# Layer 3 of a four-layer kernel: the shared expert and the second pair's projections written ahead of the expert blocks, and the sum of the state spaces kept in place

## The chip, the cores and the metric

The kernel runs on one core of a Trainium2 chip. The metric is device time in microseconds; the kernel before takes 1370.8 us, the median of three runs that reached from 1363.27 to 1372.84. "PE" is the matrix engine, "DVE" the vector engine, "ACT" the scalar engine, "POOL" the engine that also issues the indirect transfers, "SP" the queue that issues the plain ones. A matmul writes into PSUM banks[...].

## The reference, cut to what matters

Four layers follow one another on 2048 tokens of width 128. Each takes `xn = layernorm(x)`, computes a sequence mixer `s` and a gate `g` from it, and sets `x = x + s * g`. Only layer 3 is touched:

```
xn = _layernorm(x)
# mixer: two Mamba2 halves, forward on xn[:64], backward on xn[64:], 2 heads of 64, state 128
h  = rmsnorm(xn) * norm_w
zxbcdt = u @ in_w.T                      # u: one half of h
xBC = silu(conv4(xBC) + conv_b);  dt = softplus(dt + dt_bias)
scan: state = exp(dt*A)*state + (dt*x) B^T ;  y = state C
y = rmsnorm((y + D*x) * silu(z)) * gnorm_w ;  out_half = y @ outp_w.T
s = xn + concat(out_f, out_b) @ op_w.T + op_b
# gate: 16 experts of width 64, the best 2 of each token, and one shared expert of width 128
moe    = sum over the 2 best: w_k * (silu(xn @ gate_k) * (xn @ up_k)) @ down_k
shared = (silu(xn @ sh_gate.T) * (xn @ sh_up.T)) @ sh_down.T
x = x + s * silu(moe + shared)
```

The sum in `s` starts from `xn` itself, since the mixer has a residual: `s = xn + op_b + forward half + backward half`.

## The kernel before, in words

**Tiling.** Tokens lie in 16 tiles of 128 rows (`NT = 16`), four tiles to a group (`G = 4`, `NG = 4` groups), eight tiles to each of the two sequences. `x`, `xn` and `xT` (the transpose of `xn`, features on partitions) live through the whole kernel.

**Preparation (L1650 to L1685).** For each group the layer norm is written into `xn` (L1657), SP copies the group to DRAM as `xs` (`keep_rows`, L1219), ACT scales it into `xw` (L1665), POOL copies half of it (L1666), PE transposes `xn` into `xT` and `xw` into `X`, one array for each direction, shifted for the convolution. `plg` holds the router's logits and the step sizes.

**Routing (L1686 to L1693).** `top2` picks two experts of each token. `Dispatch` (L1086) turns that into blocks of 128 rows with one expert each, 47 blocks. It is a long chain of small DVE operations that ends in a large one-hot table `dhh` (L1162 on DVE, then a product on POOL, L1163), eight one-hot tables `dla` on DVE (L1170, in two buffers, borrowed from the state space's `uda`), and 32 matmuls into one bank, `pinv` (L1172, recorded as L287). From `pinv` come the row lists `dto` and `dfrom`.

**Sums.** `s` is a tile of its own in pool `a3`. POOL writes `s = xn + op_b` into it for each group (L1697). Each state-space unit later adds its output with `gated` (L1700).

**State space.** A pair is one group of tiles in both directions: `pairs[0]` to `pairs[3]`. For each pair, `stacked` computes the input projections: 24 matmuls into `px` (six banks) and 4 into `pz`, each bank followed by a SiLU on ACT into `uxs` or `usz` (L462, L472). `unit` computes the rest for one direction: `uda` -> `pd` -> exp `uE` (L545 to L548), `pe` (L557), transposes `pt`, `uxdt`, `uxst`, `pcb`, `ucb`, the product `uE` (L581), the states `pst` (L601), `py`, `pi`, `uy`, `pss`, a root (L300), `pyo`, and `gated`. `together` advances several of these generators in turn. With `busy=True` (the first three pairs) the elementwise products go to DVE, in the last pair to POOL. `uxs` has four buffers, so two pairs' projections can exist at a time.

**Blocks (L1721 to L1756).** Twelve groups of up to four blocks. For each block POOL issues an indirect gather `xb <- xs` (L1188), SP fetches the expert's weights `tw` (L1194); PE transposes (`pxb`), multiplies (`pgb`), ACT and DVE make the gated product, PE transposes (`phb`) and multiplies (`pob`), and POOL issues an indirect scatter `ys <- yb` (L1198). `xb` has two buffers of four blocks.

**Shared expert (L1757 to L1771).** For each group two matmuls of 512 columns (`pgt`, `put`), a SiLU on ACT (L1766), a product on DVE (L1767, `hT`), four matmuls into `psh`, and a copy into `acc`, which by turns goes to ACT (L282) or DVE (L284).

**End (L1774 to L1779).** For each group, `fetch` reads the two rows of each token back from `ys` (`yt`, after all scatters), adds them into `acc` on DVE (L398), then SiLU (L1776), `acc * s` (L1777), `x + acc` (L1778), and the store (L1779).

**What sets the order.** A scheduler lays out each engine's queue when the program is built: what is written earlier goes first among what it holds to be ready, and each engine then runs its queue strictly in that order, whatever is ready on the chip. PSUM banks come from two pools of four, and banks of one pool are handed out as they come free: `sa3` serves `px`, `pz`, `pc` and the units; `sf3` serves `pinv`, the blocks and the shared expert. So both streams advance side by side.

Of the kernel before, what the change touches and what calls it, by code (L numbers as in the profile page):

```python
# [10 lines left out]
F32 = mybir.dt.float32  # L11
F32R = mybir.dt.float32r
I32 = mybir.dt.int32
AF = mybir.ActivationFunctionType
# [5 lines left out]
P = 128  # L20
NB, SEQ = 2, 1024
T = NB * SEQ
NT = T // P
TPB = SEQ // P
G = 4
NG = NT // G
# [616 lines left out]
def together(*parts):  # L643

    live = list(parts)
    while live:
        live = [p for p in live if next(p, p) is not p]


def grp(a, g):  # L650
    return a[:, g * G : (g + 1) * G, :]
# [971 lines left out]
def layer3(K, x, xn, xT, w, inp, out):  # L1623
    nc, tc, c = K.nc, K.tc, K.c
    four = [P, G, P]
    with ExitStack() as es:
        pa = es.enter_context(tc.tile_pool(name="a3", bufs=1))
        pf = es.enter_context(tc.tile_pool(name="f3", bufs=1))
        sa = es.enter_context(tc.tile_pool(name="sa3", bufs=4, space=PSUM))
        sf = es.enter_context(tc.tile_pool(name="sf3", bufs=4, space=PSUM))  # L1630
# [61 lines left out]
            d = Dispatch(K, pf, pr, sf, h1, h2, 16, P, inp["lists"], ((pa, "uxs", 4, 1536), (pa, "uda", 2)))  # L1692
            w12 = K.pair_softmax(pf, m1, m2)  # L1693
        pe = es.enter_context(tc.tile_pool(name="e3", bufs=1))
        s0 = pa.tile([P, NT, P], F32, name="s")
        for g in range(NG):
            nc.gpsimd.tensor_add(grp(s0, g), grp(xn, g), w["opb"].unsqueeze(1).to_broadcast(four))  # L1697

# [12 lines left out]
        space = StateSpace(K, pa, sa, parts)  # L1711
        pairs = [[(m, b, n) for m in parts] for b in range(NB) for n in range(TPB // G)]
        together(space.stacked(pairs[0]))
        space.steps(pdt)
        together(*(space.unit(*u, busy=True) for u in pairs[0]), space.stacked(pairs[1]))
        loaded = {}

        def load_rows(n0):
# [5 lines left out]
        for n0 in range(0, d.n, 4):  # L1724
# [16 lines left out]
            sg = pf.tile([P, 4, 64], F32, name="sgb", bufs=2)[:, :m, :]  # L1741
# [8 lines left out]
            po = sf.tile(four, F32, name="pob", tag="ps")[:, :m, :]  # L1750
# [3 lines left out]
            K.copy(yb, po)  # L1754
            for r, n in enumerate(part):
                d.store(yb[:, r, :], n)  # L1756
        acc = pe.tile([P, NT, P], F32, name="acc")  # L1757
        for g in range(NG):
            rhs = xT[:, g * 512 : (g + 1) * 512]
            pgt = sf.tile([P, 512], F32, name="pgt", tag="ps")  # L1760
            put = sf.tile([P, 512], F32, name="put", tag="ps")
            K.mm(pgt, w["sg"], rhs)
            K.mm(put, w["su"], rhs)
            sg = pf.tile([P, 512], F32, name="sg", bufs=2)
            hT = pf.tile([P, 512], F32, name="hT", bufs=2)
            nc.scalar.activation(sg, pgt, AF.Silu)  # L1766
            nc.vector.tensor_mul(hT, sg, put)  # L1767
            po = sf.tile(four, F32, name="psh", tag="ps")
            for j in range(G):
                K.mm(po[:, j, :], hT[:, j * P : (j + 1) * P], w["sd"])  # L1770
            K.copy(grp(acc, g), po)  # L1771
        for n, p in enumerate(pairs[1:]):
            together(*(space.unit(*u, busy=n < 2) for u in p), *(space.stacked(q) for q in pairs[n + 2 : n + 3]))
        for g in range(NG):  # L1774
# [7 lines left out]
def build(tc, io, packs):  # L1782
    nc = tc.nc
    with ExitStack() as ctx:
        pool = ctx.enter_context(tc.tile_pool(name="const", bufs=1))
        x = pool.tile([P, NT, P], F32, name="x")
        src = io["x"].rearrange("b (t p) d -> p (b t) d", p=P)
        for g in range(NG):
            nc.sync.dma_start(grp(x, g), src[:, g * G : (g + 1) * G, :])
        xn = pool.tile([P, NT, P], F32, name="xn")  # L1790
        xT = pool.tile([P, T], F32, name="xT")

        def load(into, n, by=nc.scalar):
            t = into.tile([P, packs[n].n], F32, name="w_" + n)
            by.dma_start(t, io[n])
            return View(t, packs[n])

        K = Kern(tc, load(pool, "c"))
        dram = ctx.enter_context(tc.tile_pool(name="lists", bufs=1, space=DRAM))
        lists = {n: dram.tile([rows, P], F32, name=n) for n, rows in (("xs", T), ("ys", 2 * T))}  # L1800
        views = {}
        with tc.tile_pool(name="const0", bufs=1) as pool0:
            w0 = load(pool0, "l0")
            e0 = load(pool0, "e0")
            layer0(K, x, xn, xT, w0, e0)
        later = ctx.enter_context(tc.tile_pool(name="const3", bufs=1))
        views["l3"] = load(later, "l3")
        pair = lists["xs"], lists["ys"]
        with tc.tile_pool(name="const2", bufs=1) as pool0:
            views.update((n, load(pool0, n)) for n in ("l1", "l2"))  # L1810
            layer1(K, x, xn, xT, views["l1"], {"rows": io["rows1"], "lists": pair, **{n: io[n] for n in ("sw1", "sw3", "sw2")}})
            layer2(K, x, xn, xT, views["l2"], {"rows": io["rows2"], "lists": pair})
        layer3(K, x, xn, xT, views["l3"], {"load": lambda pool: load(pool, "x3", nc.sync), "rows": io["rows3"], "lists": pair}, io["out"].rearrange("b (t p) d -> p (b t) d", p=P))
# [17 lines left out]
```

## Time and profile before

| what | value |
|---|---|
| median of 3 runs | 1370.8 us (1363.27 to 1372.84) |
| the profiled execution | 1371.2 us, its span 1369.3 us |
| mean granted clock of PE | 0.887 |
| busy in the span: PE, DVE, ACT, POOL | 1134.2, 885.1, 634.7, 425.2 us |
| matmuls, first `px` of layer 3 | starts at 1148.0 us |
| PE between `pz` and the first `pinv` | idle for 10.05 us, from 1161.5 to 1171.5 us |
| first and last scatter or gather of layer 3 on POOL | 1181.7 and 1322.9 us |
| shared expert on PE | 1319.3 to 1342.5 us |
| last addition of a unit's output | 1363.8 us |

The span runs from the first to the last instruction, and the time is taken around it: it is 1.9 us longer in the profiled execution. Each engine's busy time is that of its own instructions; matmuls overlap, so a busy PE may still have room. A table of stretches gives for each engine the busy time within a stretch and the number of instructions, and the clock that PE was granted. In a list in order of time, a bracket says how long the engine had been idle before the line, and what released it.

### The profile page before, as it was taken

The page shows a single profiled execution, that of the slowest core. Times are in us where ns is not written, and L with a number is a line of the kernel's source. Part 1 is how long each engine was busy: PE and PEld are TensorE (multiplying, and loading weights), DVE is VectorE, ACT ScalarE, POOL GpSimd, SP SyncE. Part 2 cuts the span into 40 slices and gives each one's busy share as a digit, 9 for nine tenths or more (in the row PEclk, how much of TensorE's full clock was granted, in tenths as well). Part 3 has the DMA queues.
Part 4 walks back from the last instruction along what each step waited for, and adds up shares of the span by engine and source line. Part 5 has one row for each costly group of instructions (what it writes and reads, how often), then busy time and mean ns, then how long its engine had stood idle before and what let it go on. Part 6 is the DMA issues. An engine that isn't in the chain of part 4 may idle for free. (4 is left out here: it accounts for less than half of the span.)

```text
span 1369.3 us, 19321 instructions
## 1 busy us (share of the span) xinstructions
PE 1134.2 (83%) x6861; PEld 793.5 (58%) x6861; DVE 885.1 (65%) x2216; ACT 634.7 (46%) x1072; POOL 425.2 (31%) x420
## 2 busy tenths in 40 slices
PE   5599866888898748999999998679989918799985
PEld 2277455787798425544444433458778815577664
DVE  6536445875665686577787753988657469566456
ACT  7665926215413232344455576233452316355761
POOL 0352160027455150000000000034766521467743
PEclk9899885899999757699999998769999967799997
DMA  2000003014344200000000000024344530233411
GB/s 89 0 1 1 0 15 122 1 59 157 105 136 134 62 0 1 1 1 1 1 1 1 1 1 24 8 89 117 111 131 126 155 104 24 70 85 96 78 54 47
DMA packets 49040, 75.72 MB, mean 55 GB/s; under 512 B 7335, under 2 KB 36402, under 8 KB 48688
## 3 DMA queue, kind: packets, MB, share of 16 engines
q1 hardware_dynamic: 39632, 54.30, 12.7%
q0 software_dynamic: 8448, 14.98, 5.0%
q10 hardware_dynamic: 864, 5.21, 1.1%
q8 instruction: 54, 0.88, 0.3%
q14 instruction: 42, 0.34, 0.1%
HBM read 63.95 MB, written 12.85 MB: 56 GB/s over the span
## 5 line engine op out<-in xcount | busy, mean ns | idle before, releaser
L1424 DVE TENSOR_REDUCE mx<-pm 128x1 f32<-128x512 f32 (+3 forms) x304 | 182.1, 656 | 65.6 <-PE pm L287 62.6
L1468 ACT ACTIVATE pr<-psc 128x1024 f32<-128x1024 f32 x144 | 139.6, 1021 | 103.9 <-PE psc L287 68.2
L1188 POOL DMA_INDIRECT xb<-xs,dfrom x132 | 131.7, 998 | 123.2 <-PE pxb L797 31.5
L1198 POOL DMA_INDIRECT ys<-yb,dto x132 | 137.0, 1038 | 95.3 <-DVE yb L1076 44.4
L1163 POOL TENSOR_TENSOR dhh<-dhh,w_c 128x1280 fp32r<-128x1280 f32 (+2 forms) x3 | 8.8, 2927 | 480.3 <-issue 385.6
L287 PE MATMUL pm<-kT,qT 32*128 32x128 f32 (+3 forms) x576 | 119.3, 364 | 15.5 <-DVE mx L1424 11.4
L287 PEld LDWEIGHTS pm<-kT,qT 32*128 32x128 f32 x576 | 68.8, 203 | 68.3 <-DVE mx L1424 48.2
L287 PE MATMUL p<-xbT,tw 128*128 128x256 f32 x368 | 100.6, 391 | 1.7 <-ACT sg L1069 1.4
L1069 ACT ACTIVATE sg<-p,tw 128x256 f32<-128x256 f32 x92 | 40.8, 472 | 94.9 <-PE p L287 87.2
L287 PE MATMUL pat<-pr,va 128*32 128x512 f32 x576 | 81.0, 630 | 0.2 <-ACT pr L1468 0.2
L293 PE MATMUL tp<-w_c,xn 128*128 128x128 f32 x64 | 19.5, 412 | 67.7 <-DVE xn L325 40.3
L287 PEld LDWEIGHTS p<-xbT,tw 128*128 128x128 f32 x368 | 63.4, 194 | 12.3 <-ACT sg L1069 3.5
L287 PE MATMUL psc<-qT,kT 32*128 32x512 f32 x288 | 64.8, 487 | 3.0 <-ACT pr L1468 3.0
L1070 DVE SCALAR_TENSOR_TENSOR hh<-p,tw,sg 128x256 f32<-128x256 f32 x92 | 42.6, 479 | 35.6 <-ACT sg L1069 24.0
L287 PEld LDWEIGHTS po<-tw,hh 128*128 128x128 f32 x368 | 54.6, 193 | 5.8 <-DVE hh L1070 1.1
L287 PE MATMUL po<-tw,hh 128*128 128x128 f32 x368 | 56.7, 277 | 0.4 <-DVE hh L1070 0.4
L293 PEld LDWEIGHTS tp<-w_c,xn 128*128 128x128 f32 x64 | 11.5, 187 | 75.8 <-issue 38.7
L287 PE MATMUL psc<-mT,onesR 32*128 32x512 f32 x288 | 54.5, 410 | 0.0
L282 ACT COPY xbT<-pxb 128x256 f32<-128x256 f32 (+3 forms) x38 | 15.2, 401 | 61.0 <-PE pxb L797 44.9
L287 PEld LDWEIGHTS psc<-qT,kT 32*128 32x128 f32 x288 | 31.4, 188 | 15.9 <-ACT pr L1468 13.6
L287 PE MATMUL pcum<-kv,w_c 128*128 128x512 f32 x64 | 35.3, 652 | 2.1 <-DVE prod L1286 1.6
L287 PE MATMUL pd<-uda,w_c 128*128 128x512 f32 x64 | 34.9, 647 | 0.9 <-ACT usz L517 0.9
(531 smaller groups left out, 2840.6 us busy)
## 6 DMA issues: line engine op xcount, KB each, us to landing
tw<-in_rows SPq DMA_DIRECT2D x23, 836.0 KB, 4.8
tw<-in_rows SPq DMA_DIRECT2D x39, 384.0 KB, 3.2
yt<-ys SPq DMA_DIRECT2D x24, 256.0 KB, 3.0
tw<-in_rows SPq DMA_DIRECT2D x47, 128.0 KB, 2.2
xb<-xs,dfrom POOLq DMA_INDIRECT x132, 3.3
ys<-yb,dto POOLq DMA_INDIRECT x132, 2.3
xs<-xn SPq DMA_DIRECT2D x8, 256.0 KB, 2.3
w_l<-in_l ACTq DMA_DIRECT2D x1, 1890.0 KB, 11.1
```

What stands on the lines that cost most here:

```text
L282: self.nc.scalar.copy(out, in_)
L287: self.nc.tensor.matmul(out, lhsT=lhsT, rhs=rhs, start=start, stop=stop)
L293: self.nc.tensor.transpose(pt[:, j, :], src(g * G + j), self.c["ident"])
L1069: nc.scalar.activation(sg, p1[:, k - k0, :], AF.Silu, bias=t[:, 1536 + k : 1537 + k])
L1070: nc.vector.scalar_tensor_tensor(hh[:, k, :], p2[:, k - k0, :], t[:, 1540 + k : 1541 + k], sg, ALU.add, ALU.mult)
L1163: nc.gpsimd.tensor_mul(h, h.bitcast(F32), c["slot"][:, at].unsqueeze(2).to_broadcast(shape))
L1188: self.K.nc.gpsimd.indirect_dma_start(dst, None, self.xs, bass.IndirectOffsetOnAxis(self.of_token[:, n : n + 1], 0))
L1198: d = self.K.nc.gpsimd.indirect_dma_start(self.ys, bass.IndirectOffsetOnAxis(self.to[:, n : n + 1], 0), src, None, bounds_check=2 * T - 1, ...
L1424: nc.vector.tensor_reduce(mx[:, starts.index(a), g, j : j + k], tile[0][:, : k * m].rearrange("p (j m) -> p j m", m=m), AX.X, ALU.max)
L1468: K.nc.scalar.activation(pr, ps, AF.Exp, scale=scale)
```

## The change

Four things are changed in `layer3`, and nothing elsewhere.

1. `s0` is now `xn` itself: POOL adds `op_b` to `xn` in place, and the units add their outputs into `xn`. The tile `s` is gone.
2. `stacked(pairs[1])` was advanced together with the two units of `pairs[0]`; it is now written ahead of them, alone, right after `space.steps`.
3. The shared expert's loop is written after that, ahead of the units of `pairs[0]` and of all blocks; before, it came after the last block. Its operations are the same, in the same pool of PSUM banks.
4. `acc` comes from pool `a3` instead of `e3`, and the copy of `psh` is always ACT's.

```
-        s0 = pa.tile([P, NT, P], F32, name="s")
+        s0 = xn
         for g in range(NG):
             nc.gpsimd.tensor_add(grp(s0, g), grp(xn, g), w["opb"].unsqueeze(1).to_broadcast(four))
...
         together(space.stacked(pairs[0]))
         space.steps(pdt)
-        together(*(space.unit(*u, busy=True) for u in pairs[0]), space.stacked(pairs[1]))
+        together(space.stacked(pairs[1]))
+
+        acc = pa.tile([P, NT, P], F32, name="acc")
+        for g in range(NG):
+            rhs = xT[:, g * 512 : (g + 1) * 512]
+            pgt = sf.tile([P, 512], F32, name="pgt", tag="ps")
+            put = sf.tile([P, 512], F32, name="put", tag="ps")
+            K.mm(pgt, w["sg"], rhs)
+            K.mm(put, w["su"], rhs)
+            sg = pf.tile([P, 512], F32, name="sg", bufs=2)
+            hT = pf.tile([P, 512], F32, name="hT", bufs=2)
+            nc.scalar.activation(sg, pgt, AF.Silu)
+            nc.vector.tensor_mul(hT, sg, put)
+            po = sf.tile(four, F32, name="psh", tag="ps")
+            for j in range(G):
+                K.mm(po[:, j, :], hT[:, j * P : (j + 1) * P], w["sd"])
+            nc.scalar.copy(grp(acc, g), po)
+        together(*(space.unit(*u, busy=True) for u in pairs[0]))
         loaded = {}
...
             for r, n in enumerate(part):
                 d.store(yb[:, r, :], n)
-        acc = pe.tile([P, NT, P], F32, name="acc")
-        for g in range(NG):
-            rhs = xT[:, g * 512 : (g + 1) * 512]
...
-            K.copy(grp(acc, g), po)
         for n, p in enumerate(pairs[1:]):
```

More of the change, by code (lines that the diff above doesn't have):

```diff
@@ L1756, in layer3 @@
                 d.store(yb[:, r, :], n)
-        acc = pe.tile([P, NT, P], F32, name="acc")
-        for g in range(NG):
-            rhs = xT[:, g * 512 : (g + 1) * 512]
[L1760 to L1770, printed above, removed]
-            K.copy(grp(acc, g), po)
         for n, p in enumerate(pairs[1:]):
```

## The prediction, made before the result was known

> **What bounds the kernel now.** I first read the row of slices for PE and its clock, then a table of stretches of layer 3, then PE's, POOL's, ACT's and DVE's lists in order of time where PE was idle. The slices say that PE is the fullest engine, with dips at the layers' starts and ends; the change lies in the last six or seven slices.
>
> ```profile
> PE   5599866888898748999999998679989918799985
> PEclk9899885899999757699999998769999967799997
> ```
>
> The stretches cut layer 3 at its own events (columns: stretch; length; busy time and number for PE, weight load, DVE, ACT, POOL; PE's clock; DMA).
>
> ```profile
> 1161.50:1171.50 10.00, 0.00 (x0) 0.00 (x0) 9.83 (x23) 2.36 (x3) 3.14 (x1) 0.67 0.25 75
> 1171.50:1180.50 9.00, 8.98 (x40) 8.78 (x41) 5.35 (x8) 0.28 (x1) 0.00 (x0) 0.50 0.33 92
> 1180.50:1227.80 47.30, 45.77 (x268) 31.97 (x268) 24.59 (x59) 26.92 (x38) 31.08 (x32) 0.95 0.28 74
> 1227.80:1272.90 45.10, 42.88 (x273) 31.05 (x273) 25.81 (x59) 27.99 (x41) 32.78 (x33) 1.00 0.33 92
> 1272.90:1318.50 45.60, 42.69 (x269) 30.69 (x269) 24.89 (x62) 28.00 (x41) 32.86 (x33) 1.00 0.34 49
> 1318.50:1343.50 25.00, 21.65 (x134) 15.81 (x134) 16.52 (x40) 14.85 (x20) 11.30 (x10) 1.00 0.36 102
> 1343.50:1369.30 25.80, 11.31 (x66) 10.36 (x64) 13.49 (x39) 4.21 (x7) 5.80 (x5) 0.68 0.08 25
> ```
>
> Three things are to be seen. PE does nothing for 10 us while DVE routes. In the next 9 us it is called busy, but at half clock. From 1180.5 to 1318.5 it is busy 131.3 of 138.0 us: PE sets the pace there, with one pair's units, the next pair's projections and four block groups in each stretch. The last 51 us hold the last pair's units and the shared expert. PE's list shows the hole and its end:
>
> ```profile
> 1160.87 0.59 PE L287 MATMUL pz<-Xb,wzn 64*128 64x512 f32 x1
> 1171.51 1.90 PE L287 MATMUL pinv<-dhh,dla 128*128 128x48 f32 x8 [10.05 <-POOL dhh L1163]
> 1173.23 1.89 PE L287 MATMUL pc<-vdA,w_c 128*128 128x32 f32 x8
> 1174.94 5.55 PE L287 MATMUL pinv<-dhh,dla 128*128 128x48 f32 x24
> 1180.51 3.75 PE L287 MATMUL pd<-uda,w_c 128*128 128x512 f32 x4
> 1184.06 2.52 PE L287 MATMUL px<-Xf,fwst 128*128 128x512 f32 x4
> ```
>
> `px` at 1184 is the second pair's; its input is ready before the hole. At the end, PE's and ACT's lists show the shared expert inside the last pair's chain:
>
> ```profile
> 1331.71 1.02 PE L287 MATMUL put<-xT,w_l 128*128 128x512 f32 x2
> 1332.57 0.60 PE L567 MATMUL pt<-w_c,uxs 128*128 128x128 f32 x4
> ...
> 1341.42 1.16 PE L287 MATMUL psh<-w_l,hT 128*128 128x128 f32 x8 [0.78 <-DVE hT L1767]
> ```
> ```profile
> 1342.61 0.58 ACT L282 COPY acc<-psh 128x512 f32<-128x512 f32 x1 [3.09 <-PE psh L287]
> ```
>
> **What the Trainium skill says.** "TensorE: Matmul & The Clock Gate", Part 1, "What's actually happening": PE runs at half rate after about 3.4 us of idling and needs about as long a busy stretch to come back. The trace agrees: clock 0.50 after the hole, and four `pd` start over 3.55 us (1180.51 to 1184.06) against 1.71 us for four when warm (1321.17 to 1322.88). "ScalarE: Activation LUTs", "What ACT_TABLE_LOAD costs": every change of function set costs a load of 1283 ns; the trace has 1.28 us, seven loads ahead of `uxs` in layer 3 and two ahead of the shared expert's SiLU. "GPSIMD Engine Reference", 1. Specifications: POOL shares SBUF access with DVE operations that read two SBUF inputs; beside POOL's `dhh` product, two `dla` took 3.85 us where two alone take 1.4.
>
> **The change, part by part.** The sum is made against the profiled execution, 1371.2 us, which is 0.4 us over the runs' median.
>
> *Size of what moves.* Warm, a `px` bank takes 1.72 us (starts 1237.43, 1239.15, 1240.87): six are 10.3 us; four `pz` take 1.6 (1251.82 to 1253.42). The second pair's projections are 11.9 us of PE. A shared group is 0.85 (`pgt`) + 0.86 (`put`) + 1.09 (`psh`, 1341.42 to 1342.51) = 2.8 us; four are 11.2. Together 23.1 us.
>
> *Room beside the routing.* The hole gives 10.05 us. The stretch of `pinv` and `pc` lasts 9.0 us; 32 `pinv` warm, at the 0.53 us per four of layer 2's own `pinv` (weight loads at 903.96), are 4.2, and eight `pc` at half of 1.7 are 0.9, so 3.9 us are free. A PE that stays warm saves 1.84 us on the four `pd` and 0.63 on the four `px` at 1184 (2.35 against 1.72). Sum 16.4 us.
>
> *Before the tail.* 23.1 − 16.4 = 6.7 us of moved work are left for the stretch from 1180.5 on, where 11.9 us of `px` and `pz` lay before: the last pair starts 5.2 us earlier. Against it: with no projections beside them, the first pair's units may wait on their own chain. I take −5; bounds 0 and −8 (the 5.2 plus half of the 6.7 us of idle PE there).
>
> *The tail.* Ahead of the last pair's instructions PE has shared work of 1.8 us (1319.35 to 1321.17), 2.6 (1323.77 to 1326.39) and 3.8 with its wait (1328.75 to 1332.57): 8.2 us before the last `pt`. Then DVE's `ucb` starts 2.7 us after `pcb`'s end (1334.8, 1337.5), behind `hT` and additions into `acc`; two `hT` and one copy of `acc` (0.68 each) leave that queue. The third and fourth groups of additions waited for `acc` until 1342.6; they can follow their transfers. I take −11; bounds −6 (the additions of `yt`, 32 at 0.34 = 10.9 us, then sit in the units' way) and −13.
>
> *The blocks.* POOL issues 94 transfers at about 1.29 us, 121 us, from 1181.7. With 3.7 us of `uda` and `uwide`, and the 5.87 us wait for the first group below, it can't end before 1312; it ended at 1323.9. So it does not stop the 5 us, but a gain beyond 11 before the tail is barred.
>
> ```profile
> 1181.71 1.03 POOL L1188 DMA_INDIRECT xb<-xs,dfrom  x1 [10.26 <-DVE dfrom L1176]
> ...
> 1202.94 0.94 POOL L1188 DMA_INDIRECT xb<-xs,dfrom  x1 [5.87 <-PE pxb L1735]
> ```
>
> *Edits at or near nothing.* The in-place sum has the same four POOL additions (1.09 us) and no new DMA, but each now waits until `xn`'s readers are done: the transposes, ACT's `xw`, and SP's copy to `xs` (2.3 us to landing). Behind them on POOL stand `xw`'s copies (0.4 us), then nothing until `dhh` at 1168. Cover: POOL idles 2.6 to 3.7 us before most of these; 0 taken, +2.3 without cover. `gated` costs the same. Four `acc` copies on ACT (0.58) instead of two and two: 0; ACT is busy 0.28 of 9.0 us beside `pinv`. Four `hT` (2.7 us) come to DVE beside the `dla` chain, which leaves 3.65 of 9.0 us free: 0 taken, +2.7 if each delays a `dla`. A SiLU between exponentials there adds one or two table loads (1.3 to 2.6), on an idle ACT; the tail loses two.
>
> Sum: 1371.2 − 5 − 11 = 1355.2, so **1355 us**.
>
> **The rivals.** *The hole stays open* (chance 0.24). PE's order is fixed beforehand. `pc` needs only `vdA` (ready 1157.6), yet it stands behind eight `pinv` in the queue and so waited through the hole: the order seems to count on `dhh` earlier than the chip delivers it. If `pinv` again stands right behind the first projections, the 10 us stay, and only 3.9 + 2.5 us take moved work. Then 23.1 − 6.4 = 16.7 against 11.9: +4.8; with the tail's −11, 1365. Against: with other work ready the place of `pinv` can be chosen anew, and `pr` stood just right among `px` (ready 1155.8, run 1156.2). *The routing falls behind* (0.15), the slower case. If all 23.1 us stand ahead of `pinv` on PE, it starts at 1184.6 instead of 1171.5, 13.1 us late; so is `dfrom`, and POOL's 121 us of transfers, the last additions and the tail go with it. With 0.7 for a `hT` ahead of a `dla`: 1385. It decides once the delay of `pinv` exceeds what the tail gives back; at full passage of the delay with nothing regained it is +14. For it: the blocks' issue is near POOL's limit, so a late start isn't caught up. Against: `pinv` is written before all of it. *Only the tail gains* (0.11): the units wait on their own chain and the pace of the blocks stays: 1371.2 − 11 = 1360. That the change does nothing needs both moves to stay where they were; the new order of writing excludes that for the shared expert.
>
> **How the numbers follow.** Forecast 0.50, hole open 0.24, only the tail 0.11, routing late 0.15. The forecast's own range is 1371.2 − 8 − 13 = 1350 to 1371.2 − 6 + 2 = 1367, mostly under 1362. The range from 1345 to 1376 leaves out most of the slow case and an overshoot. One per cent, about what a measurement of this kernel can tell from no change, is 13.7 us: under 1357.1 is faster. The forecast gives 0.34 of it and the others 0.14; over 1384.5 lies two thirds of the slow case, 0.10. So 0.48, 0.42, 0.10.
>
> **What would show it.** Right: `px` of the second pair starts before `pinv`; PE idle before `pinv` under 3 us and its clock near 1.0 there; first gather within 3 us of 1181.7; the last pair's first late `pd` some 5 us before 1315; no `pgt` after 1200; `uE`'s POOL products 12 us or more before 1338.3. Wrong: `pinv` after most `pgt`, a first gather after 1186, or a last scatter later than 1323.

## The result, and the profile after

The changed kernel takes **1379.7 us**, the median of eight runs (1376.99 to 1387.01); the kernel before, beside it on the same chip, 1371.4 us, the median of eight (1363.27 to 1377.03). The ratio is 1.0078 with an interval from 1.0052 to 1.0103, so the change costs some 10.7 us (7 to 14). The two medians lie 8.3 us apart; amounts in us that stand beside a ratio below are worked out from the ratio, as here. The forecast was 1355 us in a range that ended at 1376: the sign was wrong, and the time lies above the range. The profiled execution of the changed kernel took 1387.0 us with a span of 1385.2, 7.3 us over its median. Until the first `pinv` it is no later than the one before (1171.15 against 1171.51 us), so its 15.9 us of longer span all arise after that.

The row of slices of the changed kernel, PE and its clock. Its last two slices, 7 and 4 tenths busy at a clock of 7 and 6, were 8 and 5 at 9 and 7 before: the tail has become emptier, not shorter.

```profile
PE   5699766887898658999999997689989736999974
...
PEclk9799885899999767699999998789999957999976
```

The same stretches as before, of the changed kernel; the last one is 15.9 us longer, since it reaches to the end of the span (columns: stretch; length; busy time and number for PE, weight load, DVE, ACT, POOL; PE's clock; DMA).

```profile
1161.50:1171.50 10.00, 0.35 (x2) 0.35 (x2) 9.86 (x19) 0.70 (x2) 3.15 (x1) 0.57 0.27 79
1171.50:1180.50 9.00, 9.00 (x29) 5.25 (x28) 2.22 (x4) 4.13 (x5) 0.00 (x0) 0.72 0.31 87
1180.50:1227.80 47.30, 45.82 (x287) 33.08 (x285) 26.94 (x57) 22.85 (x36) 21.60 (x22) 1.00 0.19 52
1227.80:1272.90 45.10, 42.32 (x266) 30.53 (x266) 25.51 (x58) 24.39 (x37) 32.92 (x33) 1.00 0.32 90
1272.90:1318.50 45.60, 44.30 (x280) 32.85 (x278) 24.96 (x58) 23.65 (x38) 35.77 (x36) 0.98 0.39 75
1318.50:1343.50 25.00, 18.48 (x86) 13.93 (x85) 5.58 (x19) 10.28 (x15) 10.65 (x11) 0.77 0.14 36
1343.50:1385.20 41.70, 20.03 (x108) 17.91 (x108) 27.09 (x68) 6.43 (x11) 12.15 (x10) 0.67 0.19 55
```

Three things are to be seen. PE still does nothing in the first stretch: the hole was not used. In the third stretch POOL is busy 21.6 us and not 31.1: it started its transfers later. And DVE does only 5.6 us of work in the 25 us from 1318.5, then 27.1 in the rest: the tail waits first and is crowded afterwards.

PE's list in order of time, of the changed kernel, from the last `pz` ahead of the hole to the first block:

```profile
1160.49 0.59 PE L287 MATMUL pz<-Xb,wzn 64*128 64x512 f32 x1
1171.15 1.90 PE L287 MATMUL pinv<-dhh,dla 128*128 128x48 f32 x8 [10.07 <-POOL dhh L1163]
1172.88 2.06 PE L287 MATMUL pgt<-xT,w_l 128*128 128x512 f32 x2
...
1179.14 1.88 PE L287 MATMUL px<-Xb,bwst 128*128 128x512 f32 x4
1180.45 1.37 PE L287 MATMUL pinv<-dhh,dla 128*128 128x48 f32 x8
...
1187.71 1.05 PE L287 MATMUL pinv<-dhh,dla 128*128 128x48 f32 x8
...
1193.27 1.07 PE L287 MATMUL pinv<-dhh,dla 128*128 128x48 f32 x8
...
1205.95 0.60 PE L1752 MATMUL pxb<-w_c,xb 128*128 128x128 f32 x4
```

`pinv` stands right behind `pz` as before, and waits 10.07 us. All the moved work comes behind it, most of it *between* the 32 `pinv`, which are torn into four groups of eight: the last one starts at 1194.1 us (1180.1 before). In the three gaps between the groups PE runs 17.4 us of moved work (6.7, 6.0 and 4.7 us). DVE's list shows that the tables are not what the groups wait for. `dla` has two buffers, and each is filled once its earlier content has been multiplied (the bracket gives DVE's wait for that):

```profile
1181.41 1.29 DVE L1170 TENSOR_TENSOR dla<-w_c,dlo 128x512 fp32r<-128x512 f32 x2 [3.98 <-PE pinv L287]
1188.35 1.29 DVE L1170 TENSOR_TENSOR dla<-w_c,dlo 128x512 fp32r<-128x512 f32 x2 [5.64 <-PE pinv L287]
...
1195.25 0.18 DVE L1176 TENSOR_SCALAR dfrom<-dto 128x48 int32<-128x48 int32 x1
```

The two tables begun at 1181.41 us are done at 1182.70, but PE comes to their `pinv` only at 1187.71, since projections and `psh` stand ahead of it in PE's queue; the next two are done at 1189.64 and are multiplied from 1193.27. So on the chip it is PE's order that tears `pinv`. Whether it was laid out so because `dla` has only two buffers is not shown.

The row list `dfrom` comes 14 us later, and POOL's list of the changed kernel starts there. Its first gather was at 1181.71 us before; the wait for a free buffer, 5.87 us ahead of the fourth group then, is 1.14 ahead of the third now:

```profile
1195.71 1.03 POOL L1188 DMA_INDIRECT xb<-xs,dfrom  x1 [24.61 <-DVE dfrom L1176]
...
1206.82 0.94 POOL L1188 DMA_INDIRECT xb<-xs,dfrom  x1 [1.14 <-PE pxb L1752]
```

The last scatter starts at 1336.60 us (1322.87 before). From first gather to last scatter the blocks take 140.9 us (141.2 before), so their delay of 14 us is still whole at the end. The state-space units lag less. The first `pd` of the last pair, before and in the changed kernel:

```profile
1314.98 1.88 PE L287 MATMUL pd<-uda,w_c 128*128 128x512 f32 x4
```
```profile
1322.56 1.45 PE L287 MATMUL pd<-uda,w_c 128*128 128x512 f32 x2
```

So the last pair starts 7.6 us later. From there to the end of the span it is 62.6 us (54.3 before), 8.3 more, though the shared expert has left that stretch; two block groups instead of one now stand behind this `pd` in PE's queue. From the last scatter's start to the end it is 48.6 us (46.4 before). PE's, DVE's and ACT's lists of the changed kernel there:

```profile
1339.25 1.91 PE L567 MATMUL pt<-w_c,uxs 128*128 128x128 f32 x16
1345.49 3.79 PE L287 MATMUL pcb<-uxs 128*128 128x128 f32 x16 [4.33 <-ACT uBt L572]
```
```profile
1342.11 1.14 DVE L398 SCALAR_TENSOR_TENSOR acc<-yt,rw,acc 128x128 f32<-128x128 f32 x4 [10.66 <-DMA yt<-ys]
...
1345.50 0.69 DVE L569 TENSOR_TENSOR uxdt<-pt,vdt 128x512 f32<-128x512 f32 x1
...
1354.70 0.68 DVE L578 TENSOR_TENSOR ucb<-pcb,w_c 128x512 f32<-128x512 f32 x1
```
```profile
1344.34 0.63 ACT L1778 ACTIVATE acc<-acc 128x512 f32<-128x512 f32 x1 [2.98 <-DVE acc L398]
1344.87 1.05 ACT L572 COPY uBt<-pt 128x512 f32<-128x512 f32 x2
```

`pt` runs without shared work in its way. But the next users of its banks stand behind other work: `uxdt` on DVE behind twelve additions of fetched rows, which wait 10.66 us for the rows of the last scatters, and `uBt` on ACT behind the SiLU of those sums. So `pcb` follows `pt` 6.2 us later, and takes 3.79 us after that wait. The second `ucb` comes 18.1 us after the last scatter. Before, with shared work in between, `pcb` took 1.95 us and both `ucb` ran one behind the other, from 14.7 us after the last scatter on. PE's and DVE's lines of the kernel before:

```profile
1333.01 1.95 PE L287 MATMUL pcb<-uxs 128*128 128x128 f32 x16
```
```profile
1337.52 1.28 DVE L578 TENSOR_TENSOR ucb<-pcb,w_c 128x512 f32<-128x512 f32 x2
```

### The profile page after: what moved, and what is told of

It reads as the page before. It is cut to its first block, busy times and chain, and to the rows that moved or that the text cites. A ratio compares the mean times of both kernels' runs of the same rounds, so it can differ in the third digit from the quotient of the medians.

```text
span 1385.2 us, 19307 instructions
## 1 busy us (share of the span) xinstructions
PE 1141.7 (82%) x6861; PEld 799.3 (58%) x6861; DVE 884.7 (64%) x2214; ACT 622.6 (45%) x1064; POOL 423.9 (31%) x420
## 5 line engine op out<-in xcount | busy, mean ns | idle before, releaser
L1424 DVE TENSOR_REDUCE mx<-pm 128x1 f32<-128x512 f32 (+3 forms) x304 | 182.1, 656 | 65.5 <-PE pm L287 62.5
L287 PEld LDWEIGHTS psc<-qT,kT 32*128 32x128 f32 x288 | 31.4, 188 | 15.9 <-ACT pr L1468 13.5
L545 POOL TENSOR_TENSOR uda<-w_c,vdA 128x512 f32<-128x512 f32 x20 | 20.6, 1041 | 51.3 <-PE pd L287 50.6
## 6 DMA issues: line engine op xcount, KB each, us to landing
w_l<-in_l ACTq DMA_DIRECT2D x1, 1890.0 KB, 11.2
```

The lines of the kernel that those rows point to most:

```text
L287: self.nc.tensor.matmul(out, lhsT=lhsT, rhs=rhs, start=start, stop=stop)
L545: pool.tensor_mul(da, upto.unsqueeze(1).unsqueeze(1).to_broadcast(lay), m["dA"][:, i0 + j : i0 + j + per, :].unsqueeze(3).to_broadcast(lay))
L1424: nc.vector.tensor_reduce(mx[:, starts.index(a), g, j : j + k], tile[0][:, : k * m].rearrange("p (j m) -> p j m", m=m), AX.X, ALU.max)
```

## The experiments

Every ratio is to the kernel before, run beside it on the same chip. Three readings of the loss were tested; where an expectation gives them letters, A is that the torn `pinv` alone costs the time, D that the moved work delays the first block wherever it stands ahead of it, and E that the tail does not hang on the shared expert. Milestones from each kernel's profile, in us after its own first `pinv`, which takes out what the layers ahead vary by (the first `pinv` lies between 1163.9 and 1173.6 us in these profiles; they come from three chips, on which the kernel before takes 1369 to 1372 us). "Last pair" is the start of the last pair's first `pd`, and the last column counts the block groups whose `pob` still stands behind it on PE:

| kernel | first gather | first `pxb` | last pair | last scatter | end of span | groups behind |
|---|---|---|---|---|---|---|
| before | 10.2 | 17.5 | 143.5 | 151.4 | 197.8 | 1 |
| changed | 24.6 | 34.8 | 151.4 | 165.4 | 214.0 | 2 |
| after_again (the same kernel) | 24.5 | 34.8 | 151.4 | 165.4 | 214.1 | 2 |
| only_proj | 20.8 | 24.8 | 139.0 | 172.1 | 204.4 | 3 |
| shared_inplace | 16.7 | 23.8 | 149.7 | 158.5 | 207.0 | 1 |
| after_behind | 10.2 | 39.1 | 154.5 | 188.5 | 214.4 | 3 |
| proj_behind | 10.2 | 18.2 | 145.7 | 155.1 | 201.8 | 1 |
| before_no_shared | 11.7 | 17.8 | 142.4 | 152.0 | 200.5 | 1 |

### The parts alone

*only_proj*: edit 2 alone.

```
-        together(*(space.unit(*u, busy=True) for u in pairs[0]), space.stacked(pairs[1]))
+        together(space.stacked(pairs[1]))
+        together(*(space.unit(*u, busy=True) for u in pairs[0]))
```

> Only the second pair's projections are written ahead of the first pair's units; shared expert, sums and acc stay as before. Theory A (the moved work is laid between the 32 pinv matmuls, which delays dfrom, and everything up to the end follows dfrom): PE's queue now has px and pz of the second pair between the groups of pinv, about 10 us of them, so the first gather comes at about 1189 us instead of 1181.7, the hole of 10 us ahead of pinv stays, the stretch from the first gather to the last scatter stays at 142 us, and the time is 4 to 8 us over before. Theory B (the shared expert's move alone did the harm, by its place ahead of the blocks): the first gather stays within 3 us of 1181.7 and the time is that of before or up to 5 us less.

1378.3 us, ratio 1.0039 (1.0010 to 1.0068), +5.3 us. The hole stays (10.04 us), projections lie among the `pinv`, and the last of these starts at 1191.4 us. The first block's `pxb` is 7.3 us later than before and the end 6.6. The last pair starts 4.5 us earlier than before; the loss lies behind that point, where three block groups are left instead of one (65.3 us to the end, 54.3 before).

*shared_inplace*: edits 1, 3 and 4 without edit 2.

```
-        s0 = pa.tile([P, NT, P], F32, name="s")
+        s0 = xn
...
+        acc = pa.tile([P, NT, P], F32, name="acc")
+        for g in range(NG):
+            rhs = xT[:, g * 512 : (g + 1) * 512]
...
+            nc.scalar.copy(grp(acc, g), po)
         together(*(space.unit(*u, busy=True) for u in pairs[0]), space.stacked(pairs[1]))
```

> The shared expert is written ahead, and the sums are in place; the second pair's projections stay beside the first pair's units. Theory A: pinv's groups have pgt, put and psh of three shared groups between them, some 8 us, and each waits for hT; the first gather comes at about 1188 to 1190 us, and the time is 4 to 8 us over before. Theory C (the projections alone, through the uxs buffer that dhh holds until pinv is done, did the harm): first gather within 3 us of 1181.7, time at or below before.

1378.6 us, ratio 1.0053 (1.0031 to 1.0074), +7.3 us. Here too the first block is later, by 6.3 us, and the end by 9.2. The two parts add up to 12.6 us, about what the whole change costs: neither repairs the other.

*only_inplace*: edit 1 alone (on another chip, where the kernel before takes 1422 us).

```
-        s0 = pa.tile([P, NT, P], F32, name="s")
+        s0 = xn
```

> Edit 1 alone (the sum of the state spaces kept in xn). Theory: nothing, a ratio within 0.997 to 1.003; then what the shared expert and the in-place sum together cost (7 us) is the shared expert's alone. Rival: the additions on POOL that now wait for xn's readers, and the new order around them, hold up the layer's start: +3 to +7 us, with the first pinv as much later after the layer's first px.

Ratio 0.9976 (0.9951 to 1.0001). The in-place sum costs nothing that shows; the 7.3 us above are then the shared expert's, with edit 4.

*after_again*: the changed kernel unaltered, on another chip.

> The changed kernel once more, unaltered: its first profiled execution was at 1387.0 us, 7 us above its median. Expected: a time of 1377 to 1382 us; the order of PE's queue, the hole of 10 us, the first gather 24 us and the first pxb 34 us after the first pinv as before; the end, counted from the first pinv, some 5 us or more short of the 214.0 us of that execution, if the rest of it came from the last pair's stretch or from the layers ahead.

1381.3 us, ratio 1.0092 (1.0064 to 1.0120). Its milestones equal the first profile's within 0.2 us, while its first `pinv` lies at 1165.39 us: what one profile of this kernel has more than another comes from the layers ahead. From `pinv` on the two profiles are 16 us longer than that of before, the ratios say 11 to 13; the rest is of the size of what the layers ahead vary by.

### Is it the torn `pinv`, or the work itself ahead of the first block?

*after_behind*: the changed kernel, with the moved work queued on PE behind the last `pinv`.

```
-        together(space.stacked(pairs[1]))
-
-        acc = pa.tile([P, NT, P], F32, name="acc")
+        with tc.issue_after(d.last.ins):
+            together(space.stacked(pairs[1]))
+            acc = pa.tile([P, NT, P], F32, name="acc")
...
```

> The changed kernel, with the moved projections and the shared expert queued on PE behind the last pinv matmul: the same work in the same place of the program, only pinv is whole again. Theory A: the first gather returns to 1181.7 us give or take 2, the last scatter to about 1324, and the time to that of before or up to 4 us less, so 8 us or more under the changed kernel's median of 1379.7. Theory D (PE is the limit from pinv on, so 23 us of work ahead of the blocks delays them whatever the place of pinv): the first gather is early, but the first pxb comes at 1200 or later, the stretch from first gather to last scatter grows by 8 us or more, and the time stays at 1376 or above.

1386.9 us, ratio 1.0099 (1.0075 to 1.0123), no better than the change itself. PE's and POOL's lists of this kernel:

```profile
1177.02 5.55 PE L287 MATMUL pinv<-dhh,dla 128*128 128x48 f32 x24
...
1212.72 0.60 PE L1753 MATMUL pxb<-w_c,xb 128*128 128x128 f32 x4
```
```profile
1183.79 1.03 POOL L1188 DMA_INDIRECT xb<-xs,dfrom  x1 [10.26 <-DVE dfrom L1176]
...
1213.59 1.33 POOL L1188 DMA_INDIRECT xb<-xs,dfrom  x1 [20.01 <-PE pxb L1753]
```

`pinv` is whole again and the first gather comes 10.2 us after its start, as before. But the first `pxb` now stands behind all the moved work, 39.1 us after it, and POOL waits 20 us for the buffers that `pxb` has to free: theory A is out, and the signs of D are all there. So mending `pinv` alone gives nothing as long as the same work stands ahead of the first block. Nor does the end follow the last scatter one for one: that comes 37.1 us later than before, the end 16.6.

*proj_behind*: edit 2 alone, queued in the same way.

```
-        together(*(space.unit(*u, busy=True) for u in pairs[0]), space.stacked(pairs[1]))
+        with tc.issue_after(d.last.ins):
+            together(space.stacked(pairs[1]))
+        together(*(space.unit(*u, busy=True) for u in pairs[0]))
```

> Only the second pair's projections are written ahead of the first pair's units, and on PE they are queued behind the last pinv; the shared expert and the sums are as before. With the run that moves the projections without that order (5 us median over before, first gather 20.8 us after the first pinv) it tells the torn pinv from the work ahead of the blocks. Theory A (torn pinv): first gather back to 10 us after the first pinv, time within 2 us of before or less. Theory F (only the first block's start counts): the first pxb at 20 to 24 us after the first pinv against 17.5 before, and the time 3 to 7 us over before.

1372.5 us, ratio 1.0032 (1.0013 to 1.0051), +4.4 us. First gather and first `pxb` are at before's places within 0.7 us, the end is 4 us later all the same. So the late first block is not the whole price of moving the projections: with them ahead, the first pair's units end later (58.2 us after `pinv`, 55.2 before), since nothing of the hole was won. Neither expectation is met in full: the first block is not late, and yet the time is not that of before.

*before_late_gather*: nothing moved, but the row list held on POOL (the same chip as only_inplace).

```
...
+            for _ in range(16):
+                nc.gpsimd.tensor_mul(hold, as_f.unsqueeze(1).to_broadcast(shape), one.unsqueeze(1).to_broadcast(shape))
+            nc.gpsimd.tensor_copy(self.of_token, hold[:, 7, :])
...
```

> The kernel before, with no work moved, but the row list dfrom reaches the gathers late: 16 products of 128x384 and a copy on POOL, which was idle there, stand between dfrom and the first gather, an estimated 13 to 14 us. The output is unchanged. Theory 'the first block's start sets the end': the last scatter and the end come some 10 to 14 us later, 1381 to 1385. Rival 'it is the 23 us of moved work itself, not the late first block': PE has nothing more to do here and POOL idles 5.87 us early in the gathers, so the end moves by under 4 us.

```profile
1193.66 19.38 POOL L1185 TENSOR_TENSOR dho<-def,dho 128x384 f32<-128x384 f32 x16 [10.37 <-DVE def L1179]
...
1213.94 1.03 POOL L1200 DMA_INDIRECT xb<-xs,dfrom  x1 [0.28 <-POOL dfrom L1186]
```

The products took 19.4 us, more than estimated, so the first gather is 20.4 us late. Ratio 1.0082 (1.0044 to 1.0120), +11.7 us. Late blocks alone cost as much as the whole change, with no work moved on PE. The units are not late here: counted from `pr`, a small matmul of the routing, the last pair's first `pd` starts at 195.1 us, and at 192.2 and 196.6 in only_inplace and before_busy on the same chip. The cost lies behind it, with 64.0 us to the end against 52.5 and 53.3, and with three block groups left there instead of one. Whether those groups or the additions behind the late scatters make up the 11 us is not told by this run.

### Does the tail give anything back?

*before_no_shared*: the kernel before without the shared expert.

```
         acc = pe.tile([P, NT, P], F32, name="acc")
         for g in range(NG):
-            rhs = xT[:, g * 512 : (g + 1) * 512]
...
-            K.copy(grp(acc, g), po)
+            nc.vector.memset(grp(acc, g), 0.0)
```

> The kernel before, with the shared expert left out: acc is set to zero instead, so the output lacks the shared expert's part. It measures what the shared expert costs in the tail by itself. The forecast's step for the tail (PE's 8.2 us and DVE's 2.7 us in the last pair's chain): 9 to 13 us less than before. Theory E (the tail is set by the last scatter, the transfers of yt and the additions queued around the last pair's instructions, and the shared expert lies in waits that are there anyway): 0 to 4 us less, with the stretch from the last scatter to the end still 43 to 46 us.

1373.2 us, ratio 1.0015 (0.9990 to 1.0039): taking 11.2 us of PE work and 4.1 of DVE (four `hT`, two copies of `acc`) out of the kernel gains nothing, as theory E had it. PE's and DVE's lists of its tail, whose last scatter starts at 1317.99 us:

```profile
1321.66 1.91 PE L567 MATMUL pt<-w_c,uxs 128*128 128x128 f32 x16
1326.80 3.51 PE L287 MATMUL pcb<-uxs 128*128 128x128 f32 x16 [3.23 <-DVE uxdt L569]
```
```profile
1323.30 1.14 DVE L398 SCALAR_TENSOR_TENSOR acc<-yt,rw,acc 128x128 f32<-128x128 f32 x4 [10.46 <-DMA yt<-ys]
...
1326.06 0.68 DVE L569 TENSOR_TENSOR uxdt<-pt,vdt 128x512 f32<-128x512 f32 x1
...
1333.59 0.68 DVE L578 TENSOR_TENSOR ucb<-pcb,w_c 128x512 f32<-128x512 f32 x1
```

`uxdt` stands behind the additions, which wait 10.46 us for the rows. The second `ucb` starts 15.6 us after the last scatter; before, with the shared expert, the two ran one behind the other from 14.7 us after it. The shared expert filled a wait.

*after_fetch_behind*: the changed kernel with the additions queued on DVE behind the last pair's last product, `ut` (a third chip, where the kernel before takes 1415 us; so are the next three).

```
-            nc.vector.tensor_mul(t[:, at], pi[:, at], eA[:, k, at])
+            self.late = nc.vector.tensor_mul(t[:, at], pi[:, at], eA[:, k, at])
...
-            d.fetch(pe, acc, g, w12)
+            with tc.issue_after(space.late.ins):
+                d.fetch(pe, acc, g, w12)
```

> The changed kernel, with the additions of the fetched rows, acc * s and x + acc queued on DVE behind the last pair's last product ut; nothing else is moved. Theory 'the end follows the last scatter through DVE's queue' (there uxdt, and by ACT uBt, stand behind additions that wait for the rows, which land 4.5 us after the last scatter): the pt-to-pcb wait of 4.33 us goes, ucb comes 5 to 9 us earlier, and the ratio to the kernel before is 1.000 to 1.004 instead of 1.008. Rival 'the last pair's place on PE, behind the last block, sets the end alone': at most 2 us better, 1.006 to 1.009.

Ratio 1.0046 (1.0017 to 1.0074), between what the two readings expected. The last scatter starts at 1380.53 us in this profile:

```profile
1384.07 2.51 PE L567 MATMUL pt<-w_c,uxs 128*128 128x128 f32 x16
1386.41 1.95 PE L287 MATMUL pcb<-uxs 128*128 128x128 f32 x16
...
1404.51 1.87 PE L287 MATMUL pss<-w_c,ut 128*128 128x1 f32 x8 [6.16 <-ACT ut L627]
```
```profile
1388.40 0.69 DVE L578 TENSOR_TENSOR ucb<-pcb,w_c 128x512 f32<-128x512 f32 x1 [0.20 <-PE pcb L287]
...
1395.31 3.00 DVE L398 SCALAR_TENSOR_TENSOR acc<-yt,rw,acc 128x128 f32<-128x128 f32 x7
1398.23 0.73 DVE L616 SCALAR_TENSOR_TENSOR uy<-uxs,w_l,py 128x512 f32<-128x512 f32 x1
```

The wait ahead of `pcb` is gone and the second `ucb` comes 7.9 us after the last scatter instead of 18.1. Part is lost again: the second `uy` stands behind seven additions, and `pss` waits 6.16 us for it. From the last pair's first `pd` to the end it is 52.8 us, and 50.9 in before_fetch_behind on the same chip; on the first chip, without the queueing, it is 62.6 in the changed kernel and 54.3 in the one before. So by the profiles most of what the last stretch lost is DVE's queue, whose additions stand ahead of the units' work. In the timings the cost falls from 1.0078 and 1.0092 to 1.0046, about half; the intervals overlap and the chips differ, so this share is not settled. What is left fits a last pair that starts late.

*before_fetch_behind*: the same queueing in the kernel before.

> The same queueing in the kernel before. Theory: uxdt stood 2.7 us behind its pt there, ucb 2.7 us behind pcb, uy about 3 us behind py; some of it goes: 2 to 5 us less, 0.9965 to 0.9985. Rival: the 16 us of additions after ut no longer fit in what DVE idles while the root is made, and delay ur: 0 to 5 us more.

Ratio 1.0006 (0.9978 to 1.0034). The last scatter is 44.6 us ahead of the end, against 46.4: with the shared expert in the tail, the additions were hardly in the way, and the expected 2 to 5 us are not there.

*before_busy*: the last pair's elementwise products on DVE instead of POOL, in the kernel before.

```
-            together(*(space.unit(*u, busy=n < 2) for u in p), *(space.stacked(q) for q in pairs[n + 2 : n + 3]))
+            together(*(space.unit(*u, busy=True) for u in p), *(space.stacked(q) for q in pairs[n + 2 : n + 3]))
```

> The kernel before with busy=True for the last pair too: its uda, uwide, uxst, uE and uy go to DVE instead of POOL. If POOL's products (1.09 us for 512 columns, against 0.68 on DVE) lengthen the last pair's chain: 3 to 6 us less, 1366. If DVE, which has the additions of yt there as well, is what that stretch waits for: 0 to 5 us more.

Ratio 1.0016 (0.9987 to 1.0045): moving POOL's products to DVE changes nothing that shows. Whether a gain and a loss cancel there is open.

### The hole really filled

*hole2_last*: the routing is cut ahead of `pinv`, and both pairs' projections are put into the cut, queued behind `pr`. That needs `dhh` in a tile of its own and `dla` in four buffers. The sums are in place, `acc` stays in `e3`, and the shared expert stays after the blocks.

```
+        if between:
+            between(self)
         pi = ps.tile([P, wide], F32, name="pinv", tag="ps")
...
+            def between(d):
+                first = space.stacked(pairs[0])
+                for _ in range(4):
+                    next(first)
+                with tc.issue_after(d.early.ins):
+                    together(first)
+                    space.steps(pdt)
+                    together(space.stacked(pairs[1]))
...
-        together(*(space.unit(*u, busy=True) for u in pairs[0]), space.stacked(pairs[1]))
+        together(*(space.unit(*u, busy=True) for u in pairs[0]))
```

> The routing is cut ahead of its pinv matmuls, and the second pair's projections are written into the cut, so that PE's queue holds them ahead of pinv; dhh has a tile of its own instead of one of uxs, dla has four buffers instead of two, the sums are in place, and the shared expert is written where it was before, after the blocks. Theory F (the change failed since the hole ahead of pinv stayed empty and its work went between pinv and the first block, so the first pxb slipped): PE is idle under 3 us ahead of the first pinv, pinv is whole, the first pxb is no later after the first pinv than before (17.5 us), the first pair ends about 5 us earlier than the 55 us after pinv of before, and the time is 4 to 8 us less than before. Theory G (the length after pinv is fixed by POOL's issue of transfers and by the tail): the first pair ends earlier, but the last scatter stays at 151 us or more after the first pinv and the time is within 2 us of before.

```profile
1149.76 0.38 PE L287 MATMUL pr<-dbo,dlt 128*128 128x256 f32 x1 [3.53 <-DVE dbo L1106]
...
1168.31 0.59 PE L287 MATMUL pz<-Xb,wzn 64*128 64x512 f32 x1
1168.83 3.84 PE L287 MATMUL pinv<-dhh,dla 128*128 128x48 f32 x32
1172.74 3.93 PE L287 MATMUL pd<-uda,w_c 128*128 128x512 f32 x8
```

PE works from `pr` to `pinv` without a pause, and 32 warm `pinv` take 3.84 us (the prediction had 4.2; cold, the first eight took 1.90 us in the other kernels). Yet the time is 1368.65 us against 1368.61, ratio 0.9994 (0.9974 to 1.0015). Counted from `pr`, which the kernels run when `dbo` is ready, it goes like this (a pair's sums are where the additions of its output start; the third row is the next experiment's):

| us after `pr` | first gather | first `pxb` | first pair's sums | last pair's first `pd` | last scatter | end |
|---|---|---|---|---|---|---|
| before | 25.5 | 32.8 | 70.5 | 158.8 | 166.7 | 213.1 |
| hole2_last | 24.1 | 27.6 | 51.7 | 146.5 | 180.0 | 212.0 |
| hole2_first | 24.6 | 45.7 | 61.5 | 151.0 | 187.0 | 212.4 |

The units win 19 us at first and keep 12, but the first gather, which waits for the routing, wins only 1.4. In the order laid out for this kernel three block groups, instead of one, are left behind the last pair's first `pd`. The last scatter is 13 us later, the stretch from that `pd` to the end takes 65.5 us instead of 54.3, and the gain is gone. So more room on PE brought the units forward and not the end. That it is the blocks' stream which holds the end is argued from this table, not shown, since the whole order was new.

*hole2_first*: the same with the shared expert behind the last `pinv`.

> As the run with the projections in the cut of the routing, but the shared expert is written ahead of the first pair's units and queued on PE behind the last pinv. Only the shared expert's 11 us can now stand between pinv and the first block. Theory F: the first pxb comes some 8 to 11 us later than in that run, and the time is 5 to 9 us over it, so near that of before. Theory H (the place of the shared expert is harmless as soon as pinv is whole and on time): the same time as that run within 2 us.

1366.0 us, ratio 0.9990 (0.9968 to 1.0011). The same 11.2 us of shared work cost 7.3 in shared_inplace; here they cost nothing, as theory H had it and not F. The first `pxb` comes 18.1 us later than in hole2_last and 12.9 later than before, and the end doesn't move. So a late first block is not a price by itself. One reading is that the later stretches have less to do, since projections and shared expert are both done by then; in after_behind they are too, but there, with the hole open, the first `pxb` comes only 54.2 us after `pr`. This reading was not tested.

*hole2_first_busy*: the last pair's products on DVE as well.

> hole2_first (the projections beside the routing, the shared expert behind the last pinv) with busy=True for the last pair, so that POOL has nothing but scatters between the late block groups. If the late blocks were held up by products in POOL's queue, the last scatter comes 3 to 6 us earlier and the time is 1360 to 1363, below both kernels. If the late blocks wait for PE or for DVE, it stays at 1366 to 1370.

Ratio 0.9987 (0.9947 to 1.0027): no gain shows, but the interval is too wide to exclude the one that was expected if the late blocks waited for POOL's products.

*hole2_first_fetch* and *hole2_last_fetch*: with the additions queued behind `ut`.

> hole2_first with the same queueing: projections beside the routing, the shared expert behind the last pinv, additions behind ut. Three block groups are left there for the last pair's stretch, so the last scatter is late and the additions are in the way most. Theory: 4 to 8 us less than the kernel before, 0.994 to 0.997, below both kernels. Rival (the last block on PE sets the end): 0.998 to 1.000 as without it.

> hole2_last with the same queueing; its shared expert stands in the tail. Theory: 2 to 6 us less than the kernel before, 0.996 to 0.9985, a little worse than with the shared expert ahead, since its products and copies stay in DVE's queue in the tail. Rival: as without it, 0.999 to 1.000.

Ratios 0.9990 (0.9959 to 1.0021) and 0.9978 (0.9950 to 1.0006). The second may be a gain of 3 us, which its interval doesn't settle. No version was found that is measurably below the kernel before.

## Why the prediction was wrong, by its own steps

**Size of what moves** (23.1 us): right in substance. The moved work and the `pinv` fill PE without a gap from 1171 to 1206 us.

**Room beside the routing** (16.4 us): this step failed, and with it the sign. It counted the hole's 10.05 us as room. The hole stayed at 10.07 us, and again at 10.04 to 10.06 in only_proj, proj_behind and after_behind. The queue is fixed beforehand and again has `pinv` first behind `pz`; only hole2, whose order was forced, filled it. The prediction had named the clue itself (`pc` behind eight `pinv`, ready long before) and gave it 0.24. The 3.9 us between the `pinv` were used, but at a price not in the sum: 17.4 us of moved work stand between the groups of `pinv` in PE's queue, and they delay the routing by about their length less those 3.9. That gave +14 us at the first gather. The 2.5 us of a warm PE came although the hole stayed open: eight `pc` took 1.07 us (1176.43) against 1.89, and four `pd` start over 1.82 us (1198.02 to 1199.84) against 3.55.

**Before the tail** (−5): the last pair's first `pd` starts 7.6 us later, not 5 earlier. The failed step explains most of it: without the hole, the same sum gives the +4.8 of the first rival. Where the 10 us were won, in hole2_last, the units did come 12 us earlier and the end did not, so even the true part of the step would have given nothing in that order. (The lower bound is a slip: 5.2 and half of 6.7 make −8.6, not −8.)

**The tail** (−11): measured +8.3 from that `pd` to the end. The lower bound's reason, additions in the units' way, was the fact. The prediction saw DVE's `ucb` 2.7 us behind `pcb` and blamed `hT` and copies; before_no_shared took those out and the wait for the rows stayed. It also left out that late blocks would be in the way there: two groups are left behind that `pd` instead of one. The 7.6 and 8.3 us are the 15.9 us between the two profiled spans by construction, and confirm nothing beyond them; the ratio says 7 to 14.

**The blocks**: right about the pace. POOL's stream kept its length (140.9 against 141.2 us), so a late first gather is not caught up. The prediction used this as a bar to gains only; in before_late_gather late blocks alone cost 11.7 us, by the profiles nearly all of it in the last stretch.

**Edits at nothing**: right. The in-place sum alone gave 0.9976, no cost. The first `hT` (1176.74 us) delayed no `dla`. Two table loads stand among the `pinv`, at 1175.58 and 1177.84 us, 1.28 us each, which agrees with the 1283 ns that the Trainium skill states ("ScalarE: Activation LUTs", "What ACT_TABLE_LOAD costs"); nothing late stands behind them on ACT.

**The rivals.** "The hole stays open" had the right place and nearly the right size before the tail (+4.8 against +7.6), and the wrong end, since it kept the −11. "The routing falls behind" had late `dfrom` and late transfers right and said 1385; but `pinv` is torn rather than late as a whole, and the end takes the delay over through the last stretch, not one for one. The two were held to exclude each other, and both happened. Of the marks set for a wrong forecast two showed plainly: a first gather after 1186 and a last scatter later than 1323.

**What stays open.** How the loss in the last stretch divides between DVE's queue and the block groups left on PE is known from one pair of profiles on another chip, not closer. Why the order leaves two or three block groups to that stretch was not tried, nor whether one group there would have let hole2 keep its gain.

## What to carry to other kernels

An engine's idle time is room for moved work only if the new order puts that work there: with queues fixed beforehand, ask what will stand first behind the gap, and force the order if the waiting instruction would stand there again. Work that stands in a queue among the links of a chain delays the chain by its own length, less the waits it fills. A stream that is delayed so need not delay its neighbours on the way: here it left its last pieces to the tail, and the price was paid there. Before counting work taken from a tail as a gain, look in every engine's queue for what else the next step stands behind; here it was additions waiting for a transfer.

## What the runs showed of the hardware

The chips differ more than the versions. Two of them ran the kernel before in 1415 and 1422 us, the others in 1369 to 1372; each of the slower two was used at one time only. In the table of stretches, from first `pinv` to last scatter, the kernel before on the first chip and before_busy on a slower one have about the same 871 matmuls:

```profile
1171.50:1323.90 152.40, 145.72 (x872) 105.86 (x873) 81.33 (x187) 87.53 (x125) 99.71 (x99) 0.95 0.31 71
```
```profile
1183.20:1372.00 188.80, 164.43 (x871) 121.05 (x872) 85.97 (x192) 87.74 (x125) 94.67 (x94) 0.84 0.24 57
```

The mean clock of 0.84 instead of 0.95 is not a slower clock of that size. Four warm `px` start over 1.72 us in both (1186.41 to 1188.13, and 1205.64 to 1207.36), and the clock record of either trace holds full and half rate alone. PE is idle for 24.4 us of this stretch on the slower chip, and for 6.7 on the other. ACT's, DVE's and PE's lists of before_busy show one of the places:

```profile
1242.03 0.58 ACT L282 COPY hbT<-phb 64x512 f32<-64x512 f32 x1 [5.51 <-remote]
```
```profile
1241.84 0.75 DVE L616 SCALAR_TENSOR_TENSOR uy<-uxs,w_l,py 128x512 f32<-128x512 f32 x1 [4.40 <-remote]
```
```profile
1242.66 2.07 PE L287 MATMUL pob<-tw,hbT 64*128 64x128 f32 x8 [5.00 <-ACT hbT L282]
```

Three engines stand still at once, and the profile gives the releaser as `remote`. In layer 3 of before_busy there are ten such waits on ACT and DVE; the profiles of the faster chips have none. What they wait for is not shown. So only ratios within a chip can be compared, and profiles of different chips with care.

A POOL product's time doesn't go by size alone: 128x384 took 1.21 us (19.38 for 16) in before_late_gather, while `uda` of 128x512 took 1.03 in the kernel before and `uE`, of the same size, 1.52 (6.09 for four). Nor does DVE's: four additions into `acc` took 1.14 us at 1342.11 in the changed kernel, with POOL idle, and 3.13 at 1351.04, beside POOL's `uE`.

PE came back to full pace after the hole at different times. In the kernel before, with `pinv` and `pc` of 48 and 32 columns first, four `pd` from 1180.51 us on still started over 3.55 us, 9 us and more after the hole. In the changed kernel, where matmuls of 512 columns came in from 1172.88 on, eight `pc` took 1.07 us at 1176.43, and four `px` started over 1.80 us from 1177.34.
